# Batch 0's keys by block products, a setup in an order written by hand, and output tiles in other batches: a cross-attention kernel on one core

## The chip, the core and the metric

The kernel runs on one core of one Trainium2 chip. The core has five engines that each work through their own list of instructions in order: TensorE (matrix products, PE in the profile, its weight loads PEld), VectorE (DVE), ScalarE (ACT), GpSimd (POOL) and SyncE (SP), which here only issues DMAs. Data lies in an on-chip memory of 128 partitions; products land in a second memory, PSUM, which has eight banks of 128 x 512 floats. The metric is the time of one execution on the device in microseconds; everything is in fp32.

## The reference

For each of 16 batches, x is 100 x 640 and the context 722 x 384, of which the last four rows, the tokens "ca", are kept apart. Eight heads of 80 columns:

```python
query = hidden_states @ Wq                  # 100 x 640
keyt = enc @ Wk                             # 718 x 640
valt = enc @ Wv
hs = _mha(query, keyt, valt)
ca_q1 = jnp.einsum('btc,th->bch', ca, Wq_ca)
ca_q1 = ca_q1[:, indices, :]                # 100 of 384 rows
ca_hs1 = _mha(ca_q1, residual, residual)
ca_q2 = ca_hs1 @ Wq
ca_hs2 = _mha(ca_q2, ca @ Wk_ca, ca @ Wv_ca)
out = (hs + ca_hs2) @ Wout + b_out + residual
```

`_mha` is softmax attention per head with scores scaled by 80 to the power -1/2.

## The kernel before

The host only reorders the inputs. The context of a batch is held transposed and cut into three thirds of 240 columns (KT) by three chunks of 128 channels, nine blocks in all; a weight is cut into three chunks by two column groups. A plain product of these blocks takes 3 x 3 x 2 = 18 block products. From batch 1 on keys and values are instead formed by 15 products of sums of blocks (K_PLAN and V_PLAN, lines 93 to 111: each entry names a PSUM bank A to E, a form of context and weight, and a place of the result). The sums of context blocks are made by `enc_sums` on GpSimd (line 472, 13 operations), those of weights by `weight_sums` (line 493, 12 operations per weight; the second part, "late", overwrites blocks that are still needed raw). After each product (two matmuls for keys) the bank, which goes on accumulating, is moved to its place: the first time by ScalarE's copy, later by VectorE's add (lines 394 to 398). The next product into the same bank waits for that move.

Batch 0 is different. Four of its six value blocks are formed plainly in the setup (`first_values`, line 359, called at 984), two in loop 0; its keys are formed plainly by `first_keys` (line 567), five chunks of nine matmuls. The fifth chunk of the keys (`last_keys`, line 574) is formed plainly in every batch.

The rest of the setup (lines 976 to 1090) makes, for the token path, k2 (the tokens' keys, line 991) and from it, with masks, m (line 1014: Wq's transpose times k2; one PSUM bank for each of five chunks, copied out by VectorE at 1022 and written to DRAM at 1026). `keys` (line 697) turns m into a masked m2 on GpSimd; `Second.products` (line 724) multiplies x by m2 into y, of which VectorE makes g; `scores1` (line 758) forms the first token scores on GpSimd (seven operations); `softmax1` and `exponentials1` follow on VectorE and ScalarE. Wk comes in rows and is transposed by TensorE (line 1037, bank w_ps, copied by ScalarE at 1040); Wq comes raw and is reordered by 15 VectorE copies (1048 and 1055). `va` (1069) holds the tokens' values, `queries` (line 521) the queries of two batches.

Memory is shared. kT (line 251) holds the raw Wk until the keys are written over it; wout_sb holds Wq's transpose until loop 0 loads Wout. The context buffer of batch 1 first holds the weight of va, so batch 1's context is loaded once va is done. Its two blocks in "rest" share a buffer with m's chunks 3 and 4.

PSUM has three pools of two turns each: ps2 (pairs of banks, `pair`; `bank` takes the first half of one), psk and ps1 (single banks; `psum` takes them in turn). Scores of the first and third group go to pairs, the second group's to psk and ps1.

What sets the order: the loads at the top (lines 260 to 300) are issued by SyncE in program order (`in_order`), Wv by ScalarE. In the setup a scheduler orders the engines' instructions, with a few orders forced by `issue_after`. From line 1101 (`manual_schedule`) each engine runs the loop over batches in the order in which the program is written.

In loop b the kernel forms scores, softmax and values of batch b, the keys of batch b + 1 and the token path of b + 1, in odd loops the queries of the next pair, and the output of what batch b - 1 completed: rows of all batches are cut into 13 output tiles (OC, line 33: eleven of 128 rows, one of 64, one of 128); `Last.load` (line 881) loads x for each tile that ends in this batch, `project` (line 925) multiplies by Wout, VectorE adds, SyncE writes out.

Of the kernel before, what the change touches and what calls it, by code (L numbers as in the profile page):

```python
# [18 lines left out]
P = 128  # L19
# [11 lines left out]


OC = [(r, P) for r in range(0, B * S - P - 64, P)] + [(B * S - P - 64, 64), (B * S - P, P)]
HT = NH * T

QC = [(0, 64), (64, S)]
# [32 lines left out]
RG = 4  # L69


def packed(w, c):

    if c < 4:
        lo = (c // 2) * D + 32 * (c % 2)
        return w.rearrange("(r k) n -> r k n", r=RG)[:, lo : lo + 32]
    return w.rearrange("(h k) n -> h k n", h=NH)[:, 64:]

# [46 lines left out]
def kernel(  # L125
# [69 lines left out]
    def vb_tile(name):  # L195
        return main.tile([P, T, H], F32, tag="vb", name=name)
# [80 lines left out]
            )  # L277
    load_first(0, CC, 1, slice(KN, KT))
    load_first(0, CC, 2, slice(0, KT))
    tokens = vb_tile("tokens")  # L280
    cat_sb = tokens[:, CC, : CC * B * T].rearrange("p (c n) -> p c n", c=CC)
    wkca_sb = tokens[:, :CC, :]
    in_order(nc.sync.dma_start(out=cat_sb, in_=cat.rearrange("p c b t -> p c (b t)")))
    in_order(nc.sync.dma_start(out=wkca_sb, in_=wkca.rearrange("(c p) n -> p c n", p=P)))
    wqt_sb = wout_sb
    wkt_sb = kT.rearrange("p c u k -> p c (u k)")
    in_order(nc.sync.dma_start(out=wqt_sb, in_=wqt.rearrange("(c p) r -> p c r", p=P)))
    load_first(0, CC, 0, slice(0, KT))
    xT = inp.tile([P, 2, HC, S], F32, tag="xT", name="xT_0")
    in_order(nc.sync.dma_start(out=xT, in_=xt[0:2].rearrange("b p c s -> p b c s")))  # L290
    ca_0 = small.tile([S, T, S], F32, tag="ca", name="ca_0", bufs=2)
    in_order(nc.sync.dma_start(out=ca_0, in_=cas[0].unsqueeze(0).to_broadcast([S, T, S])))
    for c in range(HC):
        in_order(nc.sync.dma_start(out=wkt_sb[:, c, :CAD], in_=packed(wkt, c)))
    halves = [t[:, u] for t in [scores_tile(f"wq_{i}") for i in range(NP)] for u in range(2)]
    room = halves.pop()
    wq_in = [t[:, :H] for t in halves]
# [192 lines left out]
        ):  # L490
            nc.gpsimd.tensor_tensor(out, left, right, op)  # L491

    def weight_sums(engine, w, late):

        at = lambda f: w[:, W_AT[f]]
        raw = lambda c, g: w[:, 2 * (c - 1) + g - 1]
        for out, left, right in (
            (at(5), raw(2, 2), raw(1, 2)),
            (at(14), raw(2, 1), raw(2, 2)),
            (at(7), raw(3, 2), at(5)),  # L500
            (at(3), raw(1, 1), at(7)),
            (at(13), raw(3, 1), at(7)),
        ) if late else (
            (at(0), raw(1, 2), raw(1, 1)),
            (at(1), raw(2, 1), raw(3, 1)),
            (at(2), raw(1, 1), raw(2, 2)),
            (at(6), raw(2, 1), raw(1, 1)),
            (at(10), raw(3, 1), raw(2, 2)),
            (at(11), raw(2, 2), raw(3, 2)),
            (at(12), raw(3, 2), raw(3, 1)),  # L510
        ):
            engine.tensor_tensor(out, left, right, ALU.subtract)


    def queries_tiles(p):
# [2 lines left out]
            for tag, n in (("qp", 2), ("qz", 1))  # L518
        ]

    def queries(p, xT, tiles, n):
        qp, qz = tiles
        q_ps = psum(f"q_ps_{p}_{n}")
        for c in range(HC):
            nc.tensor.matmul(  # L525
                q_ps[:, : 2 * S].rearrange("p (j s) -> p j s", j=2),
                wq_sb[:, c, n * P : (n + 1) * P],
                xT[:, :, c, :],
                start=(c == 0),
                stop=(c == HC - 1),  # L530
            )
# [12 lines left out]
    def chunk_keys(n, banks, weights, enc):  # L544
# [18 lines left out]
                )  # L563
            )
        return copies

    def first_keys(enc):
        for n in range(HC - 1):
            banks = [psum(f"kT_ps_0_{n}_{k}") for k in range(2)]
            weights = [wk_sb[:, 2 * c + n % 2, n // 2] for c in range(CC)]  # L570
            chunk_keys(n, banks, weights, enc)
        last_keys(0, enc)

    def last_keys(b, enc):
        banks = pair(f"kT_ps_{b}")
# [297 lines left out]
    class Last:  # L873
# [7 lines left out]
        def load(self):  # L881

            self.xn = {}
            for r, (lo, n) in enumerate(OC):
                if not self.b * S < lo + n <= (self.b + 1) * S:
                    continue
                xn = self.xn[r] = spare[1] if r == len(OC) - 1 else xn_tile(f"xn_{r}")
                rows = x.rearrange("b s n -> (b s) n")[lo : lo + n]
                for at, cols in self.parts(n):
                    to = xn[at : at + n, : cols.stop - cols.start]  # L890
                    nc.sync.dma_start(out=to, in_=rows[:, cols])
                    nc.gpsimd.tensor_tensor(to, to, bias[at : at + n, cols], ALU.add)
# [32 lines left out]
        def project(self, chunks=range(HC)):  # L925
            for r, xn in self.xn.items():
                lo, n = OC[r]
                if chunks[0] == 0:
                    self.o_ps = pair(f"o_ps_{r}")
                o_ps = self.o_ps  # L930
                for c, k in [(c, k) for k in range(2) for c in chunks]:
                    nc.tensor.matmul(  # L932
                        o_ps[:n, k, : H // 2],
                        hsTs[r][:, c, :n],
                        wout_sb[:, c, k * (H // 2) : (k + 1) * (H // 2)],
                        start=(c == 0),
                        stop=(c == HC - 1),
                    )
# [3 lines left out]
                if self.split:  # L942
                    for k in range(2):
                        cols = slice(k * (H // 2), (k + 1) * (H // 2))
                        nc.vector.tensor_tensor(
                            xn[:n, cols], o_ps[:n, k, : H // 2], xn[:n, cols], ALU.add
                        )
# [3 lines left out]
                nc.vector.tensor_tensor(both, o_ps[:n, :, : H // 2], both, ALU.add)  # L951
                nc.sync.dma_start(out=o_v, in_=xn[:n])

        def project_few(self, r):
# [25 lines left out]
        nc.tensor.matmul(idle_ps[:, :P], idle, idle, start=True, stop=True)  # L980


    for i in (1, 4, 2, 5):
        first_values(i, enc, (act, dve))


    k2_ps = psum("k2_ps")
# [11 lines left out]
    for n, heads in enumerate(HEADS):  # L999
# [8 lines left out]
            hmask[:, n, : len(heads)].unsqueeze(2).to_broadcast([P, len(heads), B * T]),  # L1008
            ALU.mult,
        )  # L1010
    for c in range(HC):
        m_ps = psum(f"m_ps_{c}")
        for n, heads in enumerate(HEADS):
# [17 lines left out]
    second.scores1()  # L1031
    keys(load_m(1))

    for c in range(HC):
        w_ps = psum(f"w_ps_{c}")
        for cc in range(CC):
            nc.tensor.transpose(
                w_ps[:, cc * P : (cc + 1) * P], wkt_sb[:, c, cc * P : (cc + 1) * P], ident
            )
        act(  # L1040
            wk_sb[:, c % 2 : 6 : 2, c // 2] if c < HC - 1 else wk4,
            w_ps[:, : CC * P].rearrange("p (a n) -> p a n", a=CC),
        )

    with tc.issue_after(summed.ins):
        for c in range(HC):
            for u in range(2):
                nc.vector.tensor_copy(
                    wq_sb[:, c, 2 * u * P : 2 * (u + 1) * P].rearrange(
                        "p (a r k) -> p a r k", a=2, r=RG  # L1050
                    ),
                    wq_in[c].rearrange("p (r k) -> p r k", r=RG)[:, :, u * D : u * D + 64]
                    .rearrange("p r (a k) -> p a r k", a=2),
                )
            nc.vector.tensor_copy(
                wq_sb[:, c, 4 * P :].rearrange("p (h k) -> p h k", h=NH),
                wq_in[c].rearrange("p (h k) -> p h k", h=NH)[:, :, 64:],
            )
    for w in wk_sb, wv_sb:
        with tc.issue_after(summed.ins):  # L1060
# [17 lines left out]
    for n in range(2):  # L1078
# [4 lines left out]
    with tc.issue_after(copied.ins):  # L1083
        nc.vector.tensor_reduce(
            qmask, ident.rearrange("p (r u k) -> p u r k", r=RG, u=2), AX.XY, ALU.add
        )
    tiles = queries_tiles(0)
    for n in range(HC):
        queries(0, xT, tiles, n)
    nc.gpsimd.dma_start(out=bias, in_=bout[0].partition_broadcast(P))  # L1090

    xT_at = [None]
    last, enc_next, second_next = None, load_rest(1, load_enc(1)), Second(1, xT)
    engines = {
        mybir.EngineType.Pool,
        mybir.EngineType.PE,
        mybir.EngineType.DVE,
        mybir.EngineType.Activation,
        mybir.EngineType.SP,
    }  # L1100
    ctx.enter_context(tc.manual_schedule(engines=engines))
    for b in range(B):
        p = b // 2
        e_in, now = enc, second
# [260 lines left out]
```

## Time and profile before

| | us |
|---|---|
| median of three runs | 953.03 (952.38 to 954.02) |
| the profiled execution | 953.95 |
| its span, first to last instruction | 952.2 |
| TensorE busy | 939.3 |
| VectorE, GpSimd, ScalarE busy | 677.3, 628.4, 362.1 |
| first score matmul of batch 0 starts | 65.68 |

The span is what the profile shows of the execution; the rest of the 953.95 lies around it. Busy shares add up over the span. The page also cuts the span into 40 slices of 23.8 us; a digit is the busy share of a slice in tenths:

```profile
PE   9899999999999999999999999999999999999998
DVE  1659795786928879496964959569793786928883
POOL 4639979576846677496773958638694576845723
DMA  8743014031130402204050040401204031120100
```

TensorE is below nine tenths in the second slice alone, apart from the ends. DMA is busiest in the first two slices, where the weights come in. In a timeline row the columns are start, duration, engine and line, operation, output and inputs, shapes, count, and in brackets the idle time before it with what ended it.

### The profile page before, as it was taken

The numbers are of one execution on the slowest core, as the hardware profiler recorded it, in microseconds if no ns is written. First come the engines' busy times: TensorE is split into PE (matmuls) and PEld (weight loads), VectorE is DVE, ScalarE is ACT, GpSimd is POOL, SyncE is SP. The second block draws the span as 40 slices with busy tenths as digits, with TensorE's granted clock in tenths as the row PEclk, the third lists the DMA queues.
The fourth block names the chain that finished last, engine by engine and source line by source line (L and its number), as shares of the span: only waits on it lengthen the run. The fifth ranks groups of instructions, "written<-read, shape, count | busy, mean of one in ns | idle before, by whom it ended". The sixth has DMA issues, their size and how long they took to land.

```text
span 952.2 us, 25609 instructions
## 1 busy us (share of the span) xinstructions
PE 939.3 (99%) x11215; PEld 799.2 (84%) x11215; DVE 677.3 (71%) x1083; ACT 362.1 (38%) x598; POOL 628.4 (66%) x570
## 2 busy tenths in 40 slices
PE   9899999999999999999999999999999999999998
PEld 6898879879898888978789787898889888898866
DVE  1659795786928879496964959569793786928883
ACT  1234442444314344343524335243431444314341
POOL 4639979576846677496773958638694576845723
PEclk9999999999999999999999999999999999999999
DMA  8743014031130402204050040401204031120100
GB/s 253 221 142 98 3 44 136 2 95 37 50 102 1 115 2 80 59 1 129 1 149 3 6 125 1 136 3 46 71 17 135 2 100 31 47 84 1 59 8 29
DMA packets 45255, 62.48 MB, mean 66 GB/s; under 512 B 13336, under 2 KB 37208, under 8 KB 43544
## 3 DMA queue, kind: packets, MB, share of 16 engines
q1 hardware_dynamic: 41608, 42.97, 15.2%
q0 software_dynamic: 2512, 16.72, 6.0%
q8 instruction: 88, 1.44, 0.6%
q10 hardware_dynamic: 1024, 1.15, 0.4%
q14 instruction: 23, 0.19, 0.1%
HBM read 55.26 MB, written 5.57 MB: 64 GB/s over the span
## 4 chain that ended last, share of the span: by engine, by line
PE 94%; DMA 3%; DVE 1%; ACT 0%; issue 0%; SPq 0%; ACTq 0%; DVEq 0%
PE s_ps L604 12%; PE a_ps L1287 12%; PE v_psA L425 10%; PE v_psB L425 8%; PE k_psA L456 7%; PE kT_ps L549 7%; PE q_ps L525 7%; PE o_ps L932 7%; PE k_psB L456 6%; PE v_psC L425 3%; PE k_psC L456 3%; PE v_psD L425 2%; PE v_psE L425 2%; PE y_ps L730 2%; DMA kT<-in_wkt 1%; PE k_psE L456 1%
## 5 line engine op out<-in xcount | busy, mean ns | idle before, releaser
L765 POOL TENSOR_TENSOR e<-ca,g 100x800 f32<-100x800 f32 x64 | 99.4, 1564 | 135.0 <-DVE most L1136 120.9
L854 POOL TENSOR_TENSOR hs<-vb,p 100x640 f32<-100x640 f32 x64 | 105.0, 1650 | 45.9 <-DVE p L840 37.9
L861 POOL TENSOR_TENSOR hs<-hs,hs 100x640 f32<-100x640 f32 x48 | 115.1, 2397 | 3.8
L1287 PEld LDWEIGHTS a_ps<-vs,st 120*64 120x64 f32 (+3 forms) x3072 | 109.1, 125 | 7.3 <-issue 5.9
L1287 PE MATMUL a_ps<-vs,st 120*64 120x81 f32 (+3 forms) x3072 | 112.3, 234 | 1.6 <-ACT st L1132 1.0
L425 PE MATMUL v_psA<-wv_sb,enc 128*120 128x320 f32 x360 | 112.0, 434 | 0.0
L1124 DVE TENSOR_TENSOR st<-st,over 120x1600 f32<-120x1600 f32 x48 | 108.2, 2255 | 0.0
L491 POOL TENSOR_TENSOR enc<-enc 128x240 f32<-128x240 f32 x135 | 101.6, 766 | 7.1
L604 PE MATMUL s_ps<-qp,kT 32*120 32x100 f32 x3072 | 98.0, 263 | 0.8 <-issue 0.8
L621 ACT COPY st<-s_ps 120x800 f32<-120x800 f32 x64 | 49.7, 829 | 126.2 <-PE s_ps L604 126.2
L604 PEld LDWEIGHTS s_ps<-qp,kT 32*120 32x120 f32 x3072 | 95.1, 179 | 2.6 <-issue 1.2
L772 POOL TENSOR_TENSOR e<-e,e 100x800 f32<-100x800 f32 x48 | 92.2, 1922 | 3.8
L425 PE MATMUL v_psB<-wv_sb,enc 128*120 128x320 f32 x300 | 93.1, 433 | 0.0
L456 PE MATMUL k_psA<-enc,wk_sb 128*128 128x240 f32 x360 | 87.6, 366 | 0.0
L1298 DVE RECIPROCAL rs<-a_ps 100x4 f32<-100x4 f32 x32 | 5.8, 182 | 113.8 <-PE a_ps L1287 113.8
L425 PEld LDWEIGHTS v_psA<-wv_sb,enc 128*120 128x120 f32 x360 | 64.5, 183 | 23.0 <-issue 0.5
L1136 DVE TENSOR_TENSOR most<-most,st 120x800 f32<-120x800 f32 x64 | 66.4, 1038 | 22.8 <-ACT st L615 21.8
L1132 ACT ACTIVATE st<-st 120x1600 f32<-120x1600 f32 x48 | 73.8, 1538 | 23.1 <-DVE st L1124 23.1
L456 PEld LDWEIGHTS k_psA<-enc,wk_sb 128*128 128x128 f32 x360 | 68.3, 190 | 16.7
L491 POOL TENSOR_TENSOR enc<-enc,rest 128x240 f32<-128x240 f32 x45 | 32.8, 729 | 73.0 <-DMA rest<-in_enct 24.9
L425 PEld LDWEIGHTS v_psB<-wv_sb,enc 128*120 128x120 f32 x300 | 54.8, 183 | 22.1 <-DVE vs L396 0.4
L456 PE MATMUL k_psB<-enc,wk_sb 128*128 128x240 f32 x300 | 73.1, 366 | 0.0
(137 smaller groups left out, 1769.4 us busy)
## 6 DMA issues: line engine op xcount, KB each, us to landing
vb<-va_d POOLq DMA_DIRECT2D x16, 1000.0 KB, 7.8
enc<-in_enct SPq DMA_DIRECT2D x30, 240.0 KB
enc<-in_enct SPq DMA_DIRECT2D x15, 360.0 KB
xT<-in_xt SPq DMA_DIRECT2D x8, 500.0 KB
rest<-in_enct SPq DMA_DIRECT2D x31, 120.0 KB
xn<-in_x SPq DMA_DIRECT2D x11, 320.0 KB
out<-xn SPq DMA_DIRECT2D x11, 320.0 KB
ca<-in_cas SPq DMA_DIRECT2D x16, 156.2 KB
```

The lines of the kernel that those rows point to most:

```text
L425: nc.tensor.matmul(at[0][j][:KN, : H // 2], a_form(self.enc, f)[:, j * KN : (j + 1) * KN], wv_sb[:, W_AT[f]], start=first, stop=last, skip ...
L456: nc.tensor.matmul(at[:, i * KT : (i + 1) * KT], wk_sb[:, W_AT[f], i], a_form(self.enc, f), start=(first and i == 0), stop=last, skip_grou ...
L491: nc.gpsimd.tensor_tensor(out, left, right, op)
L525: nc.tensor.matmul(q_ps[:, : 2 * S].rearrange("p (j s) -> p j s", j=2), wq_sb[:, c, n * P : (n + 1) * P], xT[:, :, c, :], start=(c == 0), ...
L604: nc.tensor.matmul(s_ps[r][:n, 256 * a + lo : 256 * a + hi], kT[rows, c, u, j * KN : (j + 1) * KN], rhs, start=(a == 0 and c == 0), stop=( ...
L765: first = nc.gpsimd.tensor_tensor(to, self.ca[:, t, :].unsqueeze(1).to_broadcast([S, NH, S]), g[:, :, t].unsqueeze(2).to_broadcast([S, NH, ...
L772: nc.gpsimd.tensor_tensor(e, e, to, ALU.add)
L854: first = nc.gpsimd.tensor_tensor(to, vb[:S, t, :].rearrange("p (h d) -> p h d", h=NH), p2[:, :, t].unsqueeze(2).to_broadcast([S, NH, D]), ...
L861: nc.gpsimd.tensor_tensor(sums, sums, to, ALU.add)
L1124: return nc.vector.tensor_tensor(st[i], st[i], top.over[:KN].unsqueeze(1).to_broadcast([KN, 2, ROWS]), ALU.subtract,)
L1132: nc.scalar.activation(st[i], st[i], AF.Exp, scale=SCALE)
L1287: nc.tensor.matmul(a_v[lo:hi, h % 4], st[i // 2][: KEYS[i], i % 2, h * S + lo : h * S + hi], block(i, h // 4)[: KEYS[i], h % 4], start=(i ...
```

## The change

Loads: batch 0's last context third moves ahead of the tokens, Wk ahead of Wq's transpose and in nine pieces instead of five (`load_packed`: eight of 32 partitions by two chunks, and the fifth chunk as before).

Setup: `manual_schedule` begins before the first values, so the setup too runs in the order in which it is written. `enc_sums` of batch 0 follow the first values on GpSimd. Wk's transposes move ahead of m, the early sums of Wv and all sums of Wk follow them on VectorE, ahead of m. m is copied by ScalarE. The 15 copies of Wq follow. The keys of batch 0 are formed by `Keys(0, enc)`, 15 products spread over the setup: three ahead of y, four behind it, two after each of the first four queries; `last_keys` follows the fourth query. `va_ps` and the first queries take their banks from the pairs. The bias is loaded and batch 1's masks are made behind the first token scores, and qmask is made behind them.

Output: two of the 13 tiles get another batch, those that end in batches 8 and 12 go to 9 and 13, so they are loaded and projected in loops 10 and 14 instead of 9 and 13. In the last projection each half has a bank (a pair) of its own. The order of weight sums within a list is new; the sums themselves are the same.

The diff, cut to its core:

```diff
+ENDS = [(lo + n - 1) // S for lo, n in OC]
+O_AFTER = [b + 1 if b % 2 == 0 and b + 1 not in ENDS else b for b in ENDS]
...
-def packed(w, c):
-    if c < 4:
-        lo = (c // 2) * D + 32 * (c % 2)
-        return w.rearrange("(r k) n -> r k n", r=RG)[:, lo : lo + 32]
-    return w.rearrange("(h k) n -> h k n", h=NH)[:, 64:]
+def load_packed(load, to, w):
+    rows = w.rearrange("(r u k) n -> r u k n", r=RG, u=2)
+    for r, u in [(r, u) for r in range(RG) for u in range(2)]:
+        load(
+            out=to[32 * r : 32 * r + 32, 2 * u : 2 * u + 2],
+            in_=rows[r, u, :64].rearrange("(j p) n -> p j n", j=2),
+        )
+    load(out=to[:, 4], in_=w.rearrange("(h k) n -> h k n", h=NH)[:, 64:])
...
+    load_first(0, CC, 0, slice(0, KT))
     tokens = vb_tile("tokens")
     cat_sb = tokens[:, CC, : CC * B * T].rearrange("p (c n) -> p c n", c=CC)
     wkca_sb = tokens[:, :CC, :]
     in_order(nc.sync.dma_start(out=cat_sb, in_=cat.rearrange("p c b t -> p c (b t)")))
     in_order(nc.sync.dma_start(out=wkca_sb, in_=wkca.rearrange("(c p) n -> p c n", p=P)))
+    wkt_sb = kT.rearrange("p c u k -> p c (u k)")
+    load_packed(
+        lambda **ends: in_order(nc.sync.dma_start(**ends)), wkt_sb[:, :, :CAD], wkt
+    )
     wqt_sb = wout_sb
-    wkt_sb = kT.rearrange("p c u k -> p c (u k)")
     in_order(nc.sync.dma_start(out=wqt_sb, in_=wqt.rearrange("(c p) r -> p c r", p=P)))
-    load_first(0, CC, 0, slice(0, KT))
     xT = inp.tile([P, 2, HC, S], F32, tag="xT", name="xT_0")
     in_order(nc.sync.dma_start(out=xT, in_=xt[0:2].rearrange("b p c s -> p b c s")))
     ca_0 = small.tile([S, T, S], F32, tag="ca", name="ca_0", bufs=2)
     in_order(nc.sync.dma_start(out=ca_0, in_=cas[0].unsqueeze(0).to_broadcast([S, T, S])))
-    for c in range(HC):
-        in_order(nc.sync.dma_start(out=wkt_sb[:, c, :CAD], in_=packed(wkt, c)))
...
+        for f, left, right in (
+            (0, raw(1, 2), raw(1, 1)),
+            (11, raw(2, 2), raw(3, 2)),
+            (12, raw(3, 2), raw(3, 1)),
+            (5, raw(2, 2), raw(1, 2)),
+            (7, raw(3, 2), at(5)),
+            (13, raw(3, 1), at(7)),
+            (1, raw(2, 1), raw(3, 1)),
+            (3, raw(1, 1), at(7)),
+            (6, raw(2, 1), raw(1, 1)),
+            (10, raw(3, 1), raw(2, 2)),
+            (2, raw(1, 1), raw(2, 2)),
+            (14, raw(2, 1), raw(2, 2)),
         ):
-            engine.tensor_tensor(out, left, right, ALU.subtract)
+            if late is None or late == (f in (5, 7, 13, 3, 14)):
+                engine.tensor_tensor(at(f), left, right, ALU.subtract)
...
-    def queries(p, xT, tiles, n):
+    def queries(p, xT, tiles, n, get=psum):
         qp, qz = tiles
-        q_ps = psum(f"q_ps_{p}_{n}")
+        q_ps = get(f"q_ps_{p}_{n}")
         for c in range(HC):
...
-                if not self.b * S < lo + n <= (self.b + 1) * S:
+                if self.b != O_AFTER[r]:
...
-                    self.o_ps = pair(f"o_ps_{r}")
+                if chunks[0] == 0 and self.split:
+                    self.o_ps = [bank(f"o_ps_{r}_{k}") for k in range(2)]
+                elif chunks[0] == 0:
+                    self.o_both = pair(f"o_ps_{r}")
+                    self.o_ps = [self.o_both[:, k] for k in range(2)]
                 o_ps = self.o_ps
...
+    ctx.enter_context(tc.manual_schedule(engines=engines))
     for i in (1, 4, 2, 5):
         first_values(i, enc, (act, dve))
+    enc_sums(enc)
...
+    for c in range(HC):
+        w_ps = psum(f"w_ps_{c}")
+        for cc in range(CC):
+            nc.tensor.transpose(
+                w_ps[:, cc * P : (cc + 1) * P], wkt_sb[:, c, cc * P : (cc + 1) * P], ident
+            )
+        act(
+            wk_sb[:, c % 2 : 6 : 2, c // 2] if c < HC - 1 else wk4,
+            w_ps[:, : CC * P].rearrange("p (a n) -> p a n", a=CC),
+        )
+    for c, late in ((wv_sb, False), (wk_sb, None)):
+        weight_sums(nc.vector, c, late)
...
-        copied = nc.vector.tensor_copy(
+        nc.scalar.copy(
...
     keys(load_m(0))
-    summed = second.products()
...
+    k0 = Keys(0, enc)
+    k0.go(3)
+    second.products()
     second.copy()
     second.scores1()
+    nc.gpsimd.dma_start(out=bias, in_=bout[0].partition_broadcast(P))
     keys(load_m(1))
...
-    for w in wk_sb, wv_sb:
-        with tc.issue_after(summed.ins):
-            weight_sums(nc.vector, w, False)
-    first_keys(enc)
-    weight_sums(nc.vector, wk_sb, True)
...
+    nc.vector.tensor_reduce(
+        qmask, ident.rearrange("p (r u k) -> p u r k", r=RG, u=2), AX.XY, ALU.add
+    )
+    k0.go(4)
     va = wide("va")[:, : H // 2]
-    va_ps = psum("va_ps")
+    va_ps = bank("va_ps")
     for c in range(CC):
...
-        queries(0, xT, tiles, n)
...
+        queries(0, xT, tiles, n, bank)
+        k0.go(2)
+        if n == HC - 2:
+            last_keys(0, enc)
...
```

The 15 copies of Wq stand, unchanged, ahead of `k0 = Keys(0, enc)`.

More of the change, by code (lines that the diff above doesn't have):

```diff
@@ L491, in enc_sums, with weight_sums @@
             nc.gpsimd.tensor_tensor(out, left, right, op)
-    def weight_sums(engine, w, late):
+    def weight_sums(engine, w, late=None):
         at = lambda f: w[:, W_AT[f]]
         raw = lambda c, g: w[:, 2 * (c - 1) + g - 1]
[L497 to L510, printed above, removed]
-        ):
-            engine.tensor_tensor(out, left, right, ALU.subtract)
+        for f, left, right in (
[11 more added lines that the diff above has]
+            (14, raw(2, 1), raw(2, 2)),
+        ):
+            if late is None or late == (f in (5, 7, 13, 3, 14)):
+                engine.tensor_tensor(at(f), left, right, ALU.subtract)
     def queries_tiles(p):
@@ L565, in chunk_keys @@
         return copies
[L567 to L572, printed above, removed]
     def last_keys(b, enc):
@@ L927, in project @@
                 lo, n = OC[r]
-                if chunks[0] == 0:
-                    self.o_ps = pair(f"o_ps_{r}")
+                if chunks[0] == 0 and self.split:
[3 more added lines that the diff above has]
+                    self.o_ps = [self.o_both[:, k] for k in range(2)]
                 o_ps = self.o_ps
@@ L932, in project @@
                     nc.tensor.matmul(
-                        o_ps[:n, k, : H // 2],
+                        o_ps[k][:n, : H // 2],
                         hsTs[r][:, c, :n],
@@ L945, in project @@
                         nc.vector.tensor_tensor(
-                            xn[:n, cols], o_ps[:n, k, : H // 2], xn[:n, cols], ALU.add
+                            xn[:n, cols], o_ps[k][:n, : H // 2], xn[:n, cols], ALU.add
                         )
@@ L950, in project @@
                 both = xn[:n].rearrange("p (k d) -> p k d", k=2)
-                nc.vector.tensor_tensor(both, o_ps[:n, :, : H // 2], both, ALU.add)
+                nc.vector.tensor_tensor(
+                    both, self.o_both[:n, :, : H // 2], both, ALU.add
+                )
                 nc.sync.dma_start(out=o_v, in_=xn[:n])
@@ L980 @@
         nc.tensor.matmul(idle_ps[:, :P], idle, idle, start=True, stop=True)
+    engines = {
+        mybir.EngineType.Pool,
+        mybir.EngineType.PE,
+        mybir.EngineType.DVE,
+        mybir.EngineType.Activation,
+        mybir.EngineType.SP,
+    }
+    ctx.enter_context(tc.manual_schedule(engines=engines))
     for i in (1, 4, 2, 5):
         first_values(i, enc, (act, dve))
+    enc_sums(enc)
     k2_ps = psum("k2_ps")
@@ L1028 @@
     keys(load_m(0))
-    summed = second.products()
+    for c in range(HC):
+        for u in range(2):
+            nc.vector.tensor_copy(
+                wq_sb[:, c, 2 * u * P : 2 * (u + 1) * P].rearrange(
+                    "p (a r k) -> p a r k", a=2, r=RG
+                ),
+                wq_in[c].rearrange("p (r k) -> p r k", r=RG)[:, :, u * D : u * D + 64]
+                .rearrange("p r (a k) -> p a r k", a=2),
+            )
+        nc.vector.tensor_copy(
+            wq_sb[:, c, 4 * P :].rearrange("p (h k) -> p h k", h=NH),
+            wq_in[c].rearrange("p (h k) -> p h k", h=NH)[:, :, 64:],
+        )
+    k0 = Keys(0, enc)
+    k0.go(3)
+    second.products()
     second.copy()
     second.scores1()
+    nc.gpsimd.dma_start(out=bias, in_=bout[0].partition_broadcast(P))
     keys(load_m(1))
[L1034 to L1043, printed above, removed]
-    with tc.issue_after(summed.ins):
[L1046 to L1058, printed above, removed]
-    for w in wk_sb, wv_sb:
-        with tc.issue_after(summed.ins):
-            weight_sums(nc.vector, w, False)
-    first_keys(enc)
-    weight_sums(nc.vector, wk_sb, True)
+    nc.vector.tensor_reduce(
+        qmask, ident.rearrange("p (r u k) -> p u r k", r=RG, u=2), AX.XY, ALU.add
+    )
+    k0.go(4)
     va = wide("va")[:, : H // 2]
-    va_ps = psum("va_ps")
+    va_ps = bank("va_ps")
     for c in range(CC):
@@ L1082 @@
         )
[L1083 to L1086, printed above, removed]
+    xT_at = [None]
+    last, enc_next, second_next = None, load_rest(1, load_enc(1)), Second(1, xT)
     tiles = queries_tiles(0)
     for n in range(HC):
-        queries(0, xT, tiles, n)
[L1090 to L1101, printed above, removed]
+        queries(0, xT, tiles, n, bank)
+        k0.go(2)
+        if n == HC - 2:
+            last_keys(0, enc)
     for b in range(B):
```

## The prediction

> **What bounds the kernel now.** I read the page's busy shares first, then what TensorE waited for, then the timeline of the stretches in which it waited.
>
> ```profile
> span 952.2 us, 25609 instructions
> PE 939.3 (99%) x11215; PEld 799.2 (84%) x11215; DVE 677.3 (71%) x1083; ACT 362.1 (38%) x598; POOL 628.4 (66%) x570
> ```
>
> TensorE (PE) is busy for all but 12.9 us. So time can come only from fewer or faster matmuls, and from those 12.9 us, of which this list names the largest waits:
>
> ```profile
> PE w_ps L1037 <- DMA kT<-in_wkt: 2.6, 1, 2.6
> PE hst_ps L907 <- DVE hs L1152: 1.2, 1, 1.2
> PE a_ps L1287 <- ACT st L1132: 1.0, 1, 1.0
> PE s_ps L604 <- issue: 0.8, 1, 0.8
> ```
>
> The first lies in the setup. On TensorE's timeline (start, duration, operation, idle before it):
>
> ```profile
> 22.66 6.91 PE L1014 MATMUL m_ps<-wq,wout_sb 128*128 128x128 f32 x50 [0.47 <-DVE wq L1003]
> 30.97 0.41 PE L730 MATMUL y_ps<-m,xT 128*100 128x96 f32 x2 [0.40 <-POOL m L702]
> 34.40 2.22 PE L1037 MATMUL w_ps<-ident,kT 128*128 128x128 f32 x9 [2.58 <-DMA kT<-in_wkt]
> 65.68 1.10 PE L604 MATMUL s_ps<-qp,kT 32*120 32x100 f32 x32
> ```
>
> Three waits, 0.47 + 0.40 + 2.58 = 3.45 us. The first score starts at 65.68; from there on the loop over batches runs almost without gaps, so I count how much earlier the first score can start. The table of one-microsecond stretches (last three columns: granted clock, DMA share, GB/s) shows two more things:
>
> ```profile
> 23.00:24.00 1.00, 1.00 (x9) 1.00 (x8) 0.53 (x3) 0.00 (x0) 0.00 (x0) 1.00 0.27 100
> 35.00:36.00 1.00, 1.00 (x7) 0.80 (x6) 0.00 (x0) 0.26 (x1) 1.00 (x1) 0.50 1.02 368
> ```
>
> At 22 to 25 the DMA engines are a third to a quarter busy although Wk is awaited; after the 2.58 us wait the clock is half from 34 to almost 38.
>
> **The setup, step by step.**
>
> *Products.* Batch 0's keys take 5 chunks of 9 matmuls (45 of 128x240). Afterwards 15 block products of 2 matmuls do four chunks and 9 matmuls the last: 39. In the loop four records (two matmuls) start 0.81 us apart, so six matmuls save 6 x 0.405 = **2.43 us**.
>
> *Waits.* Wk's transposes move between k2 and m. Their 15 records, about 2.1 us at full clock, cover the mask multiplications for which m waited (0.47). Three products before y cover the 0.40. Wk is loaded ahead of Wq's transpose, so the 2.58 goes if Wk is there at 22.2. Together **3.45**.
>
> *Half clock.* The nine transposes behind the wait took 2.22 instead of some 1.2, and the next six key matmul records 1.90 where later sixes take 1.38: **1.5 us**, which goes with the wait. The Trainium skill (TensorE: Matmul & The Clock Gate, Part 1) says the clock falls to half after an idle window of about 3.4 us. By that rule a 2.6 us wait would cost only itself; the trace shows it paying 1.5 more, while the waits of 1.0 and 1.2 us later leave the clock at 1.00. I go by the trace: 5.0 rather than 3.5 us from this place.
>
> *When Wk lands.* Wk has five loads of 192 KB, four with a source split as 4 x 32 rows. The row at 23 to 24 (0.27, 100 GB/s) looks like 4 of 16 engines. The skill (DMA: Bandwidth & Descriptors, Why a DMA increments its semaphore by 16 and not by 1) says a load uses the largest count up to 16 that divides the slowest dimension on both sides. By that rule the old loads get 4 engines, the eight new ones of 32 rows 16, the last (8 heads) 8. By the row alone 983 KB at 100 GB/s cost 9.8 us; at 16 engines, with the 247 to 289 GB/s of 27 to 31 us, 3.4 to 4.0. A rule of the same page speaks against the edit (Measured: batch to 1 MiB, under 64 KB a load is dominated by its descriptors): 98 KB pieces are fewer bytes per load. But from 3 to 9 us pieces of 60 to 160 KB already ran at 187 to 317 GB/s, because they overlap. I take 4 us: Wk near 17, needed at 22.2. Wq's transpose landed at 20.1 by the chain of waits; four more microseconds for Wk, less for the bias load that moves away, make 22 to 24, needed at 24.3. Hidden, with up to 0.5 us at risk. Nine issues of 0.43 us on SyncE instead of five that together took 11.4 (they waited for queue space) hold nothing up.
>
> *VectorE.* Its rows in the setup:
>
> ```profile
> 37.02 1.56 DVE L1055 COPY wq_sb<-wq 128x128 f32<-128x128 f32 x1
> 45.23 0.21 DVE L1055 COPY wq_sb<-wq 128x128 f32<-128x128 f32 x1
> 45.37 2.42 DVE L512 TENSOR_TENSOR wk_sb<-wk_sb 128x256 f32<-128x256 f32 x7
> 47.72 2.89 DVE L512 TENSOR_TENSOR wv_sb<-wv_sb 128x320 f32<-128x320 f32 x7
> ```
>
> Seven sums of Wv (2.9) and twelve of Wk (12 x 0.346 = 4.2) run from 23.5 to 30.5; m ends at 31.0, and the first product needs the fifth Wk sum. Then the 15 Wq copies, 0.21 to 0.24 each without GpSimd work (a copy beside GpSimd took 1.56): 3.5 us, to 34; GpSimd has only five mask products of 0.3 then. Queued behind them are batch 0's g and the adds of keys to kT. The adds last 0.61 to 0.66 in the loop; the first due is A3's, at 35, and the next product of its bank at 36. So the copies must not wait for Wq: by bytes (8.1 MB ahead of Wq's end at the measured 350 GB/s after 11 us) it lands at 28 to 31. Hidden.
>
> *ScalarE.* Copies of m take its free time: VectorE's row is 0.69, ScalarE's for 128x480 is 0.56; even 0.9 fits in the 1.35 us of each m chunk. *GpSimd:* 13 enc sums of 0.77, 10 us, run from about 13 to 24 in a stretch where it was idle (12.5 to 25.1). Batch 1's masks move behind scores1 and its sums follow: scores1 36 to 48, masks to 50, sums to 62, needed at 68. Six microseconds spare. Softmax 1's 7 us on VectorE now start after the last key add, at 53, and end at 61; its exponential is queued behind the first score copies at 63.5.
>
> *A new wait.* The last query bank now comes from the pairs that scores 0 need. ScalarE's two multiplications out of it take 0.75 us after the last matmul (65.79 to 66.54 before, behind which the scores ran freely). The second pair is needed by the third score matmul: **-0.95 us**. Behind the multiplications on ScalarE stand only the score copies.
>
> Setup: 2.43 + 3.45 + 1.5 - 0.95 = **6.4 us**. Check: from 22.2, transposes 2.1, m 6.7, 15 products 12.15, y 1.0, va 1.8, queries 8.65, last keys 3.65, wait 0.95 give 59.2 instead of 65.7.
>
> **The loop and the end.** Two output tiles move from batches 8 and 12 (projected in odd loops 9 and 13, which also hold queries) to loops 10 and 14, which had neither. TensorE's sum is the same. But loop 10 ends with a pause without visible releaser:
>
> ```profile
> 668.00:671.40 3.40, 3.40 (x104) 3.40 (x100) 3.19 (x6) 0.76 (x1) 0.30 (x2) 1.00 0.91 258
> 673.93 0.89 PE L604 MATMUL s_ps<-qp,kT 32*120 32x100 f32 x24 [0.80 <-issue]
> ```
>
> Its loads fill the DMA engines until 672.7, the attention matmuls follow at once, and TensorE's 16 KB instruction packet starts only at 671.5. I read the pause as late instruction fetch. Scores to y take 9.5 us here instead of 7.95: 1.6 us. With a projection of 5.4 us between loads and attention, as in every other even loop with loads, it should vanish: 0 to 1.6, I take **1.2**, nearer those other loops. In the first loop GpSimd's sums no longer run beside VectorE's maxima (1.30 and 1.20 us, against 0.99 to 1.01 in the last batch), which eases the waits of 1.0 and 1.2 us: -0.3 to 1.3, I take **0.3**, for its later maximum of 3.23 stays beside GpSimd.
>
> At the end:
>
> ```profile
> 943.80 4.50 PE L932 MATMUL o_ps<-wout_sb,spare 128*128 128x320 f32 x16
> 948.33 0.89 DVE L945 TENSOR_TENSOR spare<-o_ps,spare 128x320 f32<-128x320 f32 x2 [4.90 <-PE o_ps L932]
> ```
>
> Both adds wait for both halves. In banks of their own the first runs 1.6 us earlier; the second starts at 948.33 instead of behind it: **0.45 us**.
>
> Sum: 6.4 + 1.2 + 0.3 + 0.45, less 0.35 for small waits on landings and bank turns = **8.0 us**. The profiled execution took 953.95 us (span 952.2), 0.9 above the median; its differences are taken from the median: 953.03 - 8.0 = **945.0**.
>
> **Rivals.**
> 1. *Smaller gain, 947.5* (0.25): the fetch pause stays or appears elsewhere, and landings cost a microsecond: 8.0 - 1.2 - 1.3. For it: fetch times depend on where packets fall.
> 2. *Row groups do not spread, 952.2* (0.05): Wk at 100 GB/s puts Wq's transpose at 20.1 + 9.8 = 29.9; TensorE waits 5.7 us before m and pays 1.5 for the clock, giving back 7.2. Against: the 4-row split fits the quarter share.
> 3. *Slower, 955* (0.05): VectorE's order. If Wq lands as late as before (first copy waited until 36.25, copies done by 40 to 45), g and A3's add stand behind it, and TensorE stops before the next A product from 36 to 41 to 46, plus 1.5 of clock: 6.5 to 11.5 us lost. It is slower from copies ending after about 42. Against: that lateness came from the engines which Wk held up.
>
> The main case has 0.6 (943 to 947), a larger gain 0.05 (both pauses in full: 942.5). Range 942.4 to 949.5. A measurement of this kernel tells 0.2%, about 1.9 us, from no change. Faster 0.91, same 0.04, slower 0.05.
>
> **What would show it.** First score at 59 to 60 with a pause near 1 us behind its first matmuls, and no wait above 0.5 us from 20 to 58; the clock 1.00 throughout the setup; DMA share near 1 from 17 to 30; no pause at loop 10's end; the two last adds apart. A TensorE wait on kT in the products, or before m on wout_sb, would show rivals 3 or 2. Batches that grow longer would make the whole sum wrong.

## The result and the profile after

| | before | after |
|---|---|---|
| median of 16 runs each, us | 953.73 (951.47 to 955.67) | 950.25 (944.59 to 953.86) |
| profiled execution: time, span, us | 953.95, 952.2 | 950.02, 948.3 |
| first score matmul of batch 0, us | 65.68 | 63.47 |

The ratio of the times is 0.9967, 95% interval 0.9957 to 0.9978: faster by a third of a per cent, 3.5 us, where 8.0 were forecast. The time lies 0.8 us above the top of the range. The changed kernel's executions spread over 9 us instead of 4. Their mean granted TensorE clock goes with it: the one of 944.59 us has 1.000, the others 0.995 to 0.998.

The page of the changed kernel has nearly the same shares as before, and TensorE is busy for 3.5 us less:

```profile
span 948.3 us, 25622 instructions
PE 935.8 (99%) x11203; PEld 796.6 (84%) x11203; DVE 674.1 (71%) x1087; ACT 365.0 (38%) x601; POOL 633.0 (67%) x583
```

Then what TensorE waited for in the profiled execution of the changed kernel (total, times, longest, in us):

```profile
PE m_ps L1043 <- DMA wout_sb<-in_wqt: 3.5, 1, 3.5
PE hst_ps L909 <- DVE hs L1161: 1.3, 1, 1.3
PE a_ps L1296 <- ACT st L1141: 1.2, 1, 1.2
PE idle_ps L987 <- DVE idle L984: 1.1, 1, 1.1
PE v_ps L375 <- DMA wv_sb<-in_wv: 0.5, 1, 0.5
PE s_ps L606 <- ACT qz L546: 0.5, 1, 0.5
```

The wait for Wk (2.6 us) is down to 0.2, and a longer one for Wq's transpose, ahead of m, stands in its place. TensorE's timeline of the changed kernel (start, duration, operation, idle before it):

```profile
18.38 1.97 PE L1007 MATMUL k_ps<-tokens 128*64 128x64 f32 x60
20.28 1.20 PE L1031 MATMUL w_ps<-ident,kT 128*128 128x128 f32 x9
...
26.60 9.46 PE L1043 MATMUL m_ps<-wq,wout_sb 128*128 128x128 f32 x50 [3.51 <-DMA wout_sb<-in_wqt]
35.89 0.98 PE L465 MATMUL k_psA<-enc,wk_sb 128*128 128x240 f32 x4
...
64.38 0.98 PE L606 MATMUL s_ps<-qp,kT 32*120 32x100 f32 x26 [0.45 <-ACT qz L546]
```

m takes 9.46 us, where it took 6.91. The stretches of one microsecond (the last three columns are granted clock, DMA share and GB/s) show why, and where the load was lost:

```profile
15.00:16.00 1.00, 1.00 (x5) 0.68 (x4) 0.49 (x1) 0.00 (x0) 0.92 (x2) 1.00 1.08 147
18.00:19.00 1.00, 1.00 (x22) 0.62 (x22) 0.49 (x1) 0.00 (x0) 0.92 (x3) 1.00 0.24 63
26.00:27.00 1.00, 0.40 (x2) 0.43 (x3) 0.97 (x3) 0.00 (x0) 0.00 (x0) 0.50 1.09 375
```

From 14 to 17 the DMA engines are nearly all busy, with 147 GB/s at 15 to 16 where other loads had 350 to 400. From 17 to 20 they are two thirds to three quarters idle although Wq's transpose is awaited. The clock is half while m starts; the trace's clock records put the half clock from 25.19 to 32.02 us. SyncE's queue in the changed kernel tells what it did meanwhile (start, duration, issues):

```profile
9.19 0.43 SPq L293 DMA_DIRECT2D tokens<-in_wkca  x1
9.66 9.27 SPq L296 DMA_DIRECT2D kT<-in_wkt  x9
18.98 0.41 SPq L299 DMA_DIRECT2D wout_sb<-in_wqt  x1
```

Nine issues of Wk last until 18.9, and Wq's transpose is issued at 18.98; before, it was at 8.54. The queue's own waits say on what: `kT<-in_wkt` waited 3.9 us for the load of the tokens' weight to land. By the trace's issue records SyncE's loads take eight completion counters in turn; each load waits for the one that was issued eight places earlier. The eighth piece of Wk takes the counter of the tokens' weight and was issued at 17.80. So two things are new: the pieces move slowly, and there are more of them than places in flight.

The setup gained next to nothing. From the first matmul of the tokens' keys to the first score 45.5 us pass before (20.22 to 65.68) and 45.1 after (18.38 to 63.47), and behind the first scores stands the pause that the prediction called the new wait. What the profiled execution gained lies ahead of that stretch (1.8 us, taken up below) and behind it (2.6 us, from the running scores to the end).

The loop and the end of the changed kernel, on TensorE's and VectorE's timeline, answer to the last rows of the prediction:

```profile
663.99 6.97 PE L1296 MATMUL a_ps<-vs,st 120*64 120x81 f32 x192
670.89 1.10 PE L606 MATMUL s_ps<-qp,kT 32*120 32x100 f32 x32
...
940.19 4.50 PE L937 MATMUL o_ps<-wout_sb,spare 128*128 128x320 f32 x16
943.11 0.49 DVE L950 TENSOR_TENSOR spare<-o_ps,spare 128x320 f32<-128x320 f32 x1 [3.29 <-PE o_ps L937]
944.72 0.49 DVE L950 TENSOR_TENSOR spare<-o_ps,spare 128x320 f32<-128x320 f32 x1 [1.12 <-PE o_ps L937]
```

Loop 10's attention (to 670.9) is followed by scores at once, 32 in a row. In the kernel before, 8 came and then the pause of 0.80 us:

```profile
672.66 0.47 PE L604 MATMUL s_ps<-qp,kT 32*120 32x100 f32 x8
```

The first of the last two adds starts 1.6 us ahead of the second.

### The profile page after: what moved, and what is told of

The parts are those of the page before. It is cut to its first block, busy times and chain, and to the rows that moved or that the text cites. A ratio compares the mean times of both kernels' runs of the same rounds, so it can differ in the third digit from the quotient of the medians.

```text
span 948.3 us, 25622 instructions
## 1 busy us (share of the span) xinstructions
PE 935.8 (99%) x11203; PEld 796.6 (84%) x11203; DVE 674.1 (71%) x1087; ACT 365.0 (38%) x601; POOL 633.0 (67%) x583
## 4 chain that ended last, share of the span: by engine, by line
PE 93%; DVE 3%; DMA 2%; SPq 0%; ACT 0%; issue 0%; ACTq 0%; DVEq 0%
PE s_ps L606 12%; PE a_ps L1296 12%; PE v_psA L434 10%; PE v_psB L434 9%; PE k_psA L465 8%; PE q_ps L534 7%; PE o_ps L937 7%; PE k_psB L465 6%; PE kT_ps L558 6%; PE v_psC L434 3%; PE k_psC L465 3%; PE y_ps L732 2%; PE v_psD L434 2%; PE v_psE L434 2%; PE k_psE L465 1%; PE k_psD L465 1%
## 5 line engine op out<-in xcount | busy, mean ns | idle before, releaser
L500 POOL TENSOR_TENSOR enc<-enc 128x240 f32<-128x240 f32 x144 | 104.4, 739 | 7.5
L465 PE MATMUL k_psA<-enc,wk_sb 128*128 128x240 f32 x384 | 93.6, 366 | 0.0
L465 PEld LDWEIGHTS k_psA<-enc,wk_sb 128*128 128x128 f32 x384 | 72.6, 190 | 17.3 <-DVE kT L405 0.4
L465 PE MATMUL k_psB<-enc,wk_sb 128*128 128x240 f32 x320 | 77.9, 366 | 0.0
L500 POOL TENSOR_TENSOR enc<-enc,rest 128x240 f32<-128x240 f32 x48 | 35.7, 744 | 56.2 <-DMA rest<-in_enct 39.1
```

What stands on the lines that cost most here:

```text
L465: nc.tensor.matmul(at[:, i * KT : (i + 1) * KT], wk_sb[:, W_AT[f], i], a_form(self.enc, f), start=(first and i == 0), stop=last, skip_grou ...
```

## The experiments

The theory after the traces: Wq's transpose is late because of the form of Wk's nine pieces, and the wait is paid a second time by the half clock. The rivals: the bytes ahead of it are what counts, or m is slow for another reason. Times are medians beside runs of the kernel before on the same chip; intervals are of the ratio.

**One load of Wk.** The host puts Wk's rows in order, so that a single load of 128 partitions brings the same bytes.

```diff
-    load_packed(lambda **ends: in_order(nc.sync.dma_start(**ends)), wkt_sb[:, :, :CAD], wkt)
+    in_order(nc.sync.dma_start(
+        out=wkt_sb[:, :, :CAD], in_=wkt.rearrange("(p c) n -> p c n", c=HC)))
...
-        "wkt": np.asarray(L0_xattn_Wk).T,
+        "wkt": np.asarray(L0_xattn_Wk).T[wk_rows],
```

> The changed kernel, with Wk's rows put in order by the host, so that one load of 128 partitions x 5 x 1536 B brings it. Theory (Wk's nine pieces are slow on 32 partitions each and use up the eight places for loads in flight, so that Wq's transpose is issued at 19 us instead of about 10): Wk lands in 4 us, Wq's transpose is issued by 11 and lands near 20, m does not wait and runs at full clock (6.9 instead of 9.5 us), the first score starts about 6 us earlier than in the changed kernel, time 943 to 946 and nearly the same in each run. Rival (Wq's transpose is late because bytes ahead of it are more, whatever their form): wait before m stays above 2 us, time 948 to 951.

Measured 946.70 us, ratio 0.9931 (0.9914 to 0.9947). The profiled execution of this kernel on TensorE's timeline:

```profile
23.04 6.87 PE L1043 MATMUL m_ps<-wq,wout_sb 128*128 128x128 f32 x50 [0.24 <-ACT wk_sb L1034]
58.23 0.98 PE L606 MATMUL s_ps<-qp,kT 32*120 32x100 f32 x26 [0.45 <-ACT qz L546]
68.23 0.55 PE L794 MATMUL z_ps<-y,e 100*4 100x33 f32 x41 [2.35 <-issue]
```

and one stretch of it, with the columns of the stretches above:

```profile
15.00:16.00 1.00, 1.00 (x5) 0.67 (x4) 0.49 (x1) 0.00 (x0) 0.92 (x2) 1.00 1.06 401
```

m starts at 23.0 without waiting for a load and takes 6.87 us; the first scores come 6.15 us earlier than in the changed kernel (58.23 against 64.38). The engines move 401 GB/s where they moved 147. Bytes ahead are the same, so that rival falls. Two things were missed. The median lies above what I expected; in the trace a new pause of 2.35 us stands inside the z matmuls. And the times are not nearly the same in each run: they spread over 4.9 us. The later kernels below, which load Wk in the same way, may show one reason: in their traces m waits 0.5 to 1.5 us for Wq's transpose, which thus still lands close to the time it is needed.

**Four groups of 32 partitions.** The same source, four loads instead of one.

```diff
+    for r in range(RG):
+        in_order(nc.sync.dma_start(
+            out=wkt_sb[32 * r : 32 * r + 32, :, :CAD],
+            in_=wkt.rearrange("(p c) n -> p c n", c=HC)[32 * r : 32 * r + 32]))
```

> As the kernel with one load of Wk, but cut into four loads of 32 partitions x 5 x 1536 B. If 32 partitions as a target are what is slow, packets of 1536 B take 160 to 190 ns as in the changed kernel although only four places are used, Wk takes 7 us, and Wq's transpose, issued early, lands near 23 to 24: wait before m of 1 to 3 us, time 946 to 950. If only the places in flight count, packets take 70 to 110 ns, no wait, time as with one load.

951.87 us, ratio 0.9979 (0.9965 to 0.9994), above the 946 to 950 that I expected. Wk took 8.8 us and Wq's transpose, issued at 13.87, still came late:

```profile
23.72 1.17 PE L1033 MATMUL w_ps<-ident,kT 128*128 128x128 f32 x9 [2.35 <-DMA kT<-in_wkt]
27.96 6.84 PE L1045 MATMUL m_ps<-wq,wout_sb 128*128 128x128 f32 x50 [1.90 <-DMA wout_sb<-in_wqt]
```

A wait of 0.9 us for the tokens' weight comes on top, and the pause in the z matmuls stands here too (2.41 us, with half clock behind it). Here SyncE's queue waits for no landing between Wk and Wq's transpose, so slow pieces are enough to make it late; what the places cost by themselves was not measured. The packets of 1536 B tell why the pieces are slow. Counted over half microseconds in the traces:

| Wk's loads | packets in flight at the steadiest | ns of a packet | Wk under way, us |
|---|---|---|---|
| changed kernel: 8 of 32 partitions, 1 of 128 | 15 to 16 | 115 to 188 | 8.3 |
| one load of 128 partitions | 15 to 17 | 64 to 65 | 3.6 |
| four loads of 32 partitions | 14 to 17 | 120 to 191 | 8.8 |
| five loads as before | 4.2 | 65 | 13.2 |

Of the 8.3 us of the changed kernel a part is the 3.9 us in which the last pieces waited for a place. The packets in flight agree with the count of engines that the prediction worked with: 4 for the old loads, 16 for the new ones. But packets into 32 partitions take two to three times as long.

**Five loads as before, at the new place.** The edit is `packed` of before instead of the nine pieces.

> The changed kernel with Wk in the five loads of before (four with a source of 4 x 32 rows, one of 8 x 16), at the new place ahead of Wq's transpose. Theory: four packets in flight at 65 to 80 ns, about 100 GB/s, Wk needs 9 to 10 us, and loads behind it end late on the same engines: Wq's transpose lands at 27 or later, wait before m 4 to 6 us plus the half clock, time 950 to 955, no faster than before. If the nine pieces are the worse form, the wait is shorter than 3.5 us and the time below 950.

955.94 us, ratio 1.0023 (1.0013 to 1.0033): slower than before. Waits of 5.2 us for Wk and 3.7 us for Wq's transpose. This stretch of it shows the four engines:

```profile
17.00:18.00 1.00, 1.00 (x5) 0.66 (x4) 0.00 (x0) 0.43 (x1) 0.92 (x2) 1.00 0.26 100
```

By the two ratios (1.0023 and 0.9967) I estimate that the nine pieces are worth some 5.3 us against the five old loads at this place, and pulling Wk forward without them would have been a loss.

**A warm wait.** TensorE multiplies zeros in the stretch in which it would wait; their result is not used.

```diff
+    fill_ps = bank("fill_ps")
+    for _ in range(15):
+        nc.tensor.matmul(fill_ps[:, :P], idle, idle, start=True, stop=True)
```

> The changed kernel with 15 matmuls of zeros (128x128, no output used) on TensorE between Wk's transposes and m, about 3.4 us that fill the wait. Theory (the wait of 3.5 us costs itself and then 2.6 us, because m runs at half clock): the wait before m goes, the clock stays at 1.00, m takes 6.9 instead of 9.5 us, and the time falls by about 2.5 us to 947 to 948. Rival (m is slow for another reason, such as loads into the memory it reads): m still takes over 9 us, time as in the changed kernel or slower.

947.52 us (947.1 to 949.08), ratio 0.9940 (0.9928 to 0.9952), with Wq's transpose as late as in the changed kernel:

```profile
28.48 6.84 PE L1046 MATMUL m_ps<-wq,wout_sb 128*128 128x128 f32 x50 [0.57 <-DVE wk_sb L521]
```

Wq's transpose is issued at 20.56 here, even later than the 18.98 of the changed kernel, and yet m takes 6.84 instead of 9.46 us, at a clock of 1.00. The median is 2.7 us lower than the changed kernel's. So m's 2.6 us were the clock, and loads into the memory that it reads are not what slowed it.

**Token values later.** The pause in the z matmuls with one load of Wk had no releaser. In that trace an instruction packet of 16 KB starts at 65.83, lands at 66.93, and TensorE goes on at 68.23; ahead of it 1 MB of token values had kept the engines busy from 62 to 66 (shares of 0.57 to 0.86).

```diff
             enc_sums(enc)
-            now.load()
             now.softmax1()
...
             second.scores1()
+            now.load()
             m_next = load_m(b + 2)
```

> The kernel with one load of Wk, and in loop 0 the load of 1 MB of token values is issued behind the first token scores instead of ahead of the scores. Theory (the 2.4 us pause inside the z matmuls there is a late instruction packet, which waits behind that load): the pause goes, the time falls by up to 2 us to 944 to 945.5. Rival (the pause has another cause, such as TensorE waiting for e): it stays near 68 us, time as with one load, 946.7.

945.01 us (944.36 to 945.57), ratio 0.9905 (0.9890 to 0.9920). This interval overlaps with that of one load of Wk, so the times alone do not part the two; the trace does. The z matmuls run through, in this kernel's timeline:

```profile
66.55 0.75 PE L794 MATMUL z_ps<-y,e 100*32 100x33 f32 x64
```

The other traces support the reading as late instruction fetch. In all eleven together TensorE has twelve pauses of 0.18 to 2.41 us for which the profile names only "issue", and each of them ends 1.28 to 1.59 us after an instruction packet of 16 KB has landed (66.93 and 68.23 with one load of Wk; 672.63 and 673.93 in loop 10 of the kernel before).

**A single bank for the last query.**

```diff
-        queries(0, xT, tiles, n, bank)
+        queries(0, xT, tiles, n, bank if n < HC - 1 else psum)
```

> As the kernel before it in this list, and the last of batch 0's five query products takes a single bank instead of a pair that the scores need. Theory (the scores' third matmul waits until ScalarE has multiplied out of that bank): the wait of 0.5 us behind the first four score matmuls goes and the first scores run without the gap of 0.9 us, time 0.9 us less. Rival: the wait moves to the product with the masked queries, no gain.

944.25 us (943.36 to 945.46), ratio 0.9897 (0.9883 to 0.9911): 0.76 us below the one before it, too near to its spread to be sure from the times. The trace is clear on the wait: the scores start at 57.78 and run without the gap, and there is no wait on `qz` any more. But a pause without releaser (0.69 us at 62.05) now stands among them. This version has the lowest median of the study, 9.7 us below the kernel before in its own comparison; its interval overlaps with those of the version before it and of the five wide loads below.

**Plain keys.** On top of that kernel, the first four chunks without products: `plain(n)` calls `chunk_keys` at four places, and the context sums go.

> As the kernel with the single query bank, but batch 0's first four key chunks are formed plainly, 36 matmuls instead of 30, without the context sums ahead and with the late sums of Wk behind the fourth chunk. Theory (a matmul of 128x240 is worth 0.405 us): first score 2.4 us later, time 2.4 us more. Rival (the products lose part of their gain to VectorE's moves between them): less than 1.5 us more.

946.24 us (945.36 to 947.35), 2.0 us more. In the traces the first score moves from 57.78 to 60.19, which is 2.41 us. Of these, 0.27 us are a later start of m (23.79 against 23.52); from there to the first score the plain keys take 2.14 us more, where six matmuls at 0.405 make 2.43. So the products keep most of their gain, and the rival falls.

**Output as before.** On top of the kernel with the single bank, `O_AFTER = ENDS`, and one pair for the last projection.

> As the kernel with the single query bank, but all output tiles in the loops of before and the last projection in one pair of banks. Theory: the pause at the end of loop 10 comes back (about 1.0 us, and slower scores behind it, 1.6 us in all), and the end is 0.45 us longer: time 1.5 to 2 us more. Rival (that pause was a matter of this one execution): only the 0.45 us of the end.

948.24 us (947.0 to 949.35), 4.0 us more, where I had expected 1.5 to 2; the spans of the two profiled executions differ by 2.8. At the end of loop 10 this kernel shows the pause again, and half clock behind it (second row, with the columns of the stretches above):

```profile
667.02 0.93 PE L606 MATMUL s_ps<-qp,kT 32*120 32x100 f32 x11 [1.72 <-issue]
668.00:669.00 1.00, 1.00 (x22) 1.00 (x20) 0.00 (x0) 0.00 (x0) 1.00 (x2) 0.50 0.06 16
```

It comes and goes with the moved tiles in every trace kept, so it was no accident of one execution. The half clock, from 666.98 to 670.39, is what I had left out: I estimate 1.7 us for it, half of that stretch. Tiles and banks went back together, so the times do not part them. From the end of the last matmul to the end of the span 4.2 us pass here and 3.6 with two banks (3.9 in the kernel before, 3.6 in the changed kernel).

**Five wide loads.** To part "cut in pieces" from "few partitions": five loads, each of one chunk, into all 128 partitions.

```diff
+    for c in range(HC):
+        in_order(nc.sync.dma_start(out=wkt_sb[:, c, :CAD], in_=wkt[c * P : (c + 1) * P]))
```

> As the kernel with one load of Wk, but in five loads, one for each chunk, of 128 partitions x 1536 B from one contiguous stretch of 196 KB. Theory (it is the 32 partitions as a target that slow the packets, not the cutting): packets of 1536 B take 65 to 75 ns, Wk lands in 4 us, Wq's transpose is issued by 14 us, wait before m below 1.5 us, time 945 to 948. Rival (several small loads from narrow stretches of memory are slow in any form): packets above 110 ns, Wk takes 6 us or more, time 949 to 952, as with four groups.

944.55 us (943.42 to 947.03), ratio 0.9912 (0.9886 to 0.9939). Packets take 65 to 66 ns nearly all the while that Wk is under way, and the wait before m is short:

```profile
PE m_ps L1042 <- DMA wout_sb<-in_wqt: 0.7, 1, 0.7
```

Five pieces do no harm; 32 partitions as a target do. Which part of the path to those partitions is full was not tried, nor were nine wide pieces, which would show what the places cost alone.

## Why the prediction was wrong

*The step that failed* is "When Wk lands". The engines were counted rightly, but their rate was taken from loads into 128 partitions: 3.4 to 4.0 us for Wk instead of the 8.3 that it was under way. So "Hidden, with up to 0.5 us at risk" was 3.5 us of waiting, and 2.6 more for m at half clock. Beside it, "Nine issues ... hold nothing up" failed: it counted the time of an issue, and not that SyncE's loads here wait for the eighth before them to land. Its own sentence had the sign: the five issues of before "waited for queue space". Together 6.1 us were lost at this place, more than the 4.5 between forecast and result. With one load of Wk, m does not wait for a load in the trace shown and the median is 946.7; with the fetch pause of that kernel taken away too it is 945.0. That this is the very time forecast is chance: it is 9.0 us below the kernel before in its own comparison, where 8.0 were forecast, and with a change that the forecast did not have.

That the result lies so near the range is chance as well. Up to the running scores the prediction put 6.4 us; the two profiles show 1.3 (65.68 and 64.38), of which 1.8 came before the step that failed; behind it 0.5 was lost. The loop and the end gave 2.6 us where it put 1.6.

What happened is rival 2 in mechanism, Wq's transpose late behind Wk and the clock paid in addition, at about its price (7.2 against 6.1 us), with 0.05 of the chance. Its cause was named wrongly: the groups do spread.

*Products*, 2.43: 2.14 from m to the first score, right but for 0.3. *Old waits*, 3.45: gone but for 0.5 in two short ones ahead of m (0.29 and 0.22); right.

*Half clock*: it was right to go by the trace, and the half clock behind the old wait is gone. What I left out is that a new wait can pay the same surcharge: 2.6 us for the 3.5, shown by the warm wait. Nor does the length of a wait alone decide: the pause of 1.72 us in loop 10 brought half clock with the output as before, and the one of 2.35 us with one load of Wk did not (the last section says why).

*VectorE and GpSimd*: the Wq copies end at 34.8, g is due at 39.5; nothing waits in the products. Right.

*The new wait* of 0.95: the scores go on at 64.38, 0.91 after the start, but 0.45 of that is the first four matmuls; 0.45 us is idle, and undoing it brought some 0.8 in the medians, near their spread. Right in kind, put too high.

*Loop 10*, 1.2: the changed kernel runs from attention to scores without a pause, and undoing the tiles brings it back; right, and rather larger than put, since the pause can bring half clock. *The end*, 0.45: 0.3 to 0.6; right. *First loop*, 0.3: the waits are 1.2 and 1.3 where they were 1.0 and 1.2. Nothing was eased; wrong, and small. *The larger gain* does not come out of its own terms: both pauses in full add 0.4 and 1.0 to 8.0, which makes 943.6 and not 942.5.

*Rival 1* said that a fetch pause may appear elsewhere. In the changed kernel's profile none does; it did with one load of Wk (2.35 us) and with four groups (2.41 us).

Not settled: in the profiled execution of before the first values end at 20.2, in the changed kernel's at 18.4, with the same matmuls. In the former the matmuls from 4.8 to 8 us ran at half the later pace. The clock records agree: full clock begins at 10.16 us in the execution of before, and between 4.71 and 6.91 in the ten others. So 1.8 of the 2.2 us by which the first score came earlier may not be the change's. One execution of before is shown; whether the start differs as a rule is open.

## What to carry to other kernels

When a load is cut so that more engines work on it, look at both ends: how many partitions the pieces write to, and how many places in flight they take from the loads behind them. A load moved forward has to be priced with what it delays, and a wait of TensorE of some 1.7 us or more with its clock as well: as a risk, since it depends on where the wait falls. And a stretch with few long matmuls behind a burst of loads is where a late instruction packet shows, so a shorter setup can move that pause rather than remove it.

## What the runs showed of the hardware

Sixteen engines with packets of 1536 B took 65 ns for each into 128 partitions, and 115 to 191 ns into 32, from sources of similar size (196 and 245 KB a load). SyncE's loads in this program used eight counters in turn. In the four pauses behind a burst of loads (0.8 to 2.4 us) TensorE went on 1.3 to 1.4 us after an instruction packet of 16 KB had landed; with the load moved away, the one tried was gone.

TensorE's clock changed on a grid of 3.41 us. In each of the eleven traces the times between its changes are whole multiples of that: with the output as before, full clock from 4.79 us and half clock from 666.98 are 194 steps apart. The half clock lasted one step in the kernel before, with four groups and with the output as before, two in the changed kernel (25.19 to 32.02), three with the five old loads at the new place (25.46 to 35.70).

What counts is the idle time of TensorE within one step. Ahead of the five falls between the first and the last matmul it was 2.6 us (before), 2.3 (changed kernel), 2.3 (four groups, the pause), 2.9 (five old loads) and 1.67 (output as before). In no trace did a step at full clock with more than 1.69 us of it leave the clock whole, so the edge lies near 1.7. The pause of 2.35 us with one load of Wk lay across two steps, 1.0 and 1.3 us, and left the clock whole.
